# Four fused image layers on one core: new orders for copies, output products and the first loads

## The chip, the core and the metric

The kernel runs on one core of a Trainium2 chip. The metric is the device time of one execution in microseconds, the median of the runs. Everything is in 32-bit floats.

## What is computed

An input x of 4 batches, 512 channels and 64 x 64 places goes through four layers in turn. Cut to what matters:

```python
# layer 0: attention over the 4096 places, 64 channels of keys, queries and values
t = einsum('oc,bchw->bohw', w_qkv, x)
attn = softmax(einsum('bdk,bdq->bkq', key, query), axis=1)
x = scale * einsum('oc,bchw->bohw', w_out, einsum('bdk,bkq->bdq', value, attn)) + x
# layer 1: a router mixes 8 experts' weights for each batch; 1x1, 3x3 and 1x1 convolutions
rw = sigmoid(x.mean(axis=(2, 3)) @ router_w.T + router_b)
x = relu(bn(conv1(relu(bn(conv3(relu(bn(conv1(x)))))))) + x)
# layer 2: linear attention with softplus features
Q, K, V = softplus(Wq x + bq), softplus(Wk x + bk), Wv x + bv
x = x + gamma * (Q (K V)) / (Q . (sum K + 1e-6))
# layer 3: gate and scan; discounted running sums down the columns, then along the rows
gate, scan = split(w_proj x + b_proj)
x = x + gamma * gate * sigmoid(ds_cumsum(ds_cumsum(scan, d, 2), d, 3))
```

## The kernel before, in words

**Tiles.** A batch is held in SBUF as four *pairs*, tiles `x` of 128 partitions x 4 channel groups x 1024 places (2 MB each). The four batches run one after the other through `layer0` to `layer3` (loop at the end of `unshifted`). TensorE's order is the order of the program (`manual_schedule` for PE round that loop). In some scopes VectorE's or ScalarE's order is that of the program as well; elsewhere a scheduler orders their instructions by its own estimate of what is ready. In what follows "group" is a turn of the attention loop and "batch" one of the four images.

**Loads at the start.** `load_pair` (L86) loads a pair: for batch 0 the pairs 0 and 1 by channel group, four DMAs of 512 KB each (L91 to L93), the pairs 2 and 3 in one DMA of 2 MB (L95). Ahead of them SyncE issues the projection weights `wqkv_sb` (L100) and the parameters `prm_sb` (L102), behind them the other constants.

**Stage one of attention** (`Projections`, L213 to L338) makes keys, queries and values. For keys and queries it uses Strassen's seven products for two pairs at once; the lists in `steps` (L230) give the order, one list for the pairs (0, 1), one for (2, 3). The steps: a digit is one of the seven products on TensorE (eight matmul instructions, L305): 1, 6, 7 and 4 add up in the bank `y` (in the profile `kq`), 5 and 3 in the second half of `zy` (`kqz`), 2 in its first half. `seed` (L310) copies y into zy's first half, so that 2 adds to it; `e2` and `e3` (L313) copy y out in between. `c11` copies zy's first half into the key tile by four ScalarE copies (L291), `c22` (L327) and `c12` (L319) are VectorE's sums of zy's second half with e3 and e2, `c21` (L325) copies y to the queries. `t5` to `t4` and `n5` to `n4` are VectorE's differences of x that the products take (L253), t for this list, n for the next pairs. `v0` to `v3` are value products of a pair (16 instructions, L261); `v3a` and `v3b` are halves of one. `cp` copies values out (L267), `tr` transposes them (L274), `k` copies the second pair's keys to the other partitions. `zero` (L298) is a product of the identity whose result `seed` overwrites, put ahead of the first products while x is on its way.

**Attention** (L446 to L470): 16 groups, 0 to 15, four for each pair of queries. A group makes eight score tiles on TensorE (L367), each in one of three PSUM buffers (`pair_psum`, shared with all other two-bank tiles), ScalarE's exponentials into a ring of 12 tiles (L370), VectorE's running sum `acc` of them (L375, each waiting for the one before), and eight value products (`av`, L382), half a group behind. When a pair's last value product is done, its `sums` (`den` L398, reciprocal L401, `o` L410 or L412, range statistics L419 and L420) go into the list `late`, and for pairs 0 and 1 four output steps too (`y` L426, addition L431), each with the first group in which it may run. At the end of each group up to two of the list's items are taken (L468). Pair 3's own `den` is placed by hand, ahead of the value product with the index 121 of 128 (L456: `NPAIR * NT - 7`).

**Layer 2** leaves a rest in the list `left` (L830): the query features of the pairs 2 and 3, their `softplus` (L673: ScalarE's Abs, Relu, Exp, VectorE's +1, ScalarE's Ln, then `softplus_end`), and a division.

**Layer 3** works on eight tiles of two channel blocks by 1024 places. A tile has seven products for the scanned half (`s1` to `s7`) and, one turn later, seven for the gates (`g1` to `g7`), again in Strassen's way (L920), with ScalarE's copies in between (`seed` L925, `copy_out` L929, `first` L938, `third` L945). The scan of the tile before (`l`) runs beside: `rows` (VectorE, L953), `turn` (ScalarE, L959), `columns` (VectorE, L966 and L970), `sigmoid` (ScalarE, L975 and L976). The order is a list of rows: `first_steps` for the first tile, `steps` for the others, `last_steps`, and `end_steps` for the last batch's end. In a row `y` is the next output product of layer 2 (L838), `a` its addition to x (L843), `q` takes an item from `left`, `t` makes sums of x for the next pair or batch, `d` sets a scan constant.

**The range test** (L1114 to L1123) follows all batches: four small VectorE instructions on the statistics of all reciprocals, a product with ones (L1122), a conversion (L1123). Every engine then reads the result `fits` (L1514) and branches over the slower, general program (L1515).

The order of stage one, and the loop's end:

```python
first = "v1 cp01 5 1 seed v2 t6 t4 n5 6 n6 e2 2 7 e3 c22 c11 tr01 n7 4 c21 3 c12 n4"
if b == 0:
    first = "zero v0 1 seed t5 v1 cp01 t6 5 2 t7 t4 6 e2 v2 7 e3 n5 c22 c11 tr01 n6 n7 4 c21 3 c12 n4"
return first.split(), "5 1 seed k v3a 6 e2 2 v3b cp23 7 e3 c22 c11 tr23 4 c21 3 c12".split()
```

Of the kernel before, what the change touches and what calls it, by code (L numbers as in the profile page):

```python
# [15 lines left out]
P = 128  # L16
# [4 lines left out]
KC = C // P  # L21
# [25 lines left out]
def unshifted(ctx: ExitStack, tc: tile.TileContext, fits, x, wqkv_t, wout_t, router_t,  # L47
# [38 lines left out]
    def load_pair(b, pr):  # L86
        if b and pr == NPAIR - 1:
            places[NPAIR - 1:] = places[NPAIR], places[NPAIR - 1]
        t = places[pr]
        src = x[b, :, pr * 2 * NB:(pr + 1) * 2 * NB].rearrange("(kc p) n -> p kc n", p=P)  # L90
        if b == 0 and pr < 2:  # L91
            for kc in range(KC):
                nc.sync.dma_start(t[:, kc, :], src[:, kc, :])  # L93
        else:
            nc.sync.dma_start(t, src)  # L95
        return t
# [3 lines left out]
    nc.sync.dma_start(wqkv_sb, wqkv_t.rearrange("(kc p) o -> p kc o", p=P))  # L100
    prm_sb = const.tile([P, NPRM], F32, tag="prm", name="prm_sb")
    nc.sync.dma_start(prm_sb, prm)  # L102
# [110 lines left out]
    class Projections:  # L213
# [16 lines left out]
        def steps(self, b):  # L230
            first = "v1 cp01 5 1 seed v2 t6 t4 n5 6 n6 e2 2 7 e3 c22 c11 tr01 n7 4 c21 3 c12 n4"
            if b == 0:
                first = "zero v0 1 seed t5 v1 cp01 t6 5 2 t7 t4 6 e2 v2 7 e3 n5 c22 c11 tr01 n6 n7 4 c21 3 c12 n4"
            return first.split(), "5 1 seed k v3a 6 e2 2 v3b cp23 7 e3 c22 c11 tr23 4 c21 3 c12".split()
# [47 lines left out]
        def products(self, xs, pair, steps, key, qry, vt):  # L282
# [10 lines left out]
            for step in steps:  # L293
                if y is None and (step.isdigit() or step == "zero"):
                    y, zy = bank(f"kq_{self.b}_{pair[0]}"), pair_psum(f"kqz_{self.b}_{pair[0]}")
                if step == "zero":

                    nc.tensor.matmul(zy[:, 0, :].rearrange("p (j c) -> p j c", c=P), ident,  # L298
                                     ident[:, None, :].to_broadcast([P, TPB, P]), start=True, stop=True)
                elif step.isdigit():  # L300
                    k = int(step)
                    to = y if k in (1, 6, 7, 4) else zy[:, 0 if k == 2 else 1, :]
                    for c in range(2):
                        for h in range(2):
                            nc.tensor.matmul(to[h * D:(h + 1) * D, :], self.w[k][:, c, :],  # L305
                                             self.term(xs, pair, k, c)[:, h * NB:(h + 1) * NB],
                                             start=c == 0 and k in (1, 5), stop=c == 1,
                                             skip_group_check=k not in (1, 5))
                elif step == "seed":
                    nc.scalar.copy(zy[:, 0, :], y)  # L310
                elif step in ("e2", "e3"):
                    e[step] = block(f"{step}_{self.b}_{pair[0]}")
                    nc.scalar.copy(e[step], y)  # L313
                elif step == "c11":
                    to_key(lambda h, n0: zy[h * D:(h + 1) * D, 0, :], pair[0])
                elif step == "c12":
                    for h in range(2):
                        r, n0 = slice(h * D, (h + 1) * D), (2 * pair[1] + h) * NB
                        nc.vector.tensor_tensor(key[r, n0:n0 + NB], zy[r, 1, :], e["e2"][r, :], ALU.add)  # L319
                    self.left.append(lambda: to_key(lambda h, n0: key[h * D:(h + 1) * D, n0:n0 + NB], pair[1],  # L320
                                                    own=False))
                elif step == "k":
                    self.key_copies()
                elif step == "c21":
                    nc.vector.tensor_copy(qry[:, pair[0] * NB:(pair[0] + 1) * NB], y)  # L325
                elif step == "c22":
                    nc.vector.tensor_tensor(qry[:, pair[1] * NB:(pair[1] + 1) * NB], zy[:, 1, :], e["e3"], ALU.add)  # L327
                elif step[0] in "tn" and step[1].isdigit():
                    for c in range(2):
                        self.sum(xs, pair if step[0] == "t" else (2, 3), int(step[1]), c)  # L330
                elif step[:2] == "cp":
                    self.value_copy(int(step[2]) // 2)
                elif step[:2] == "tr":
                    self.value_turn(int(step[2]) // 2, vt)
                elif step[2:] == "a" or step[2:] == "b":
                    self.value(xs, int(step[1]), 0 if step[2] == "a" else 2, 2)
                else:
                    self.value(xs, int(step[1]))  # L338

    def layer0(b, xs, pro):  # L340
# [106 lines left out]
        with tc.manual_schedule(engines={mybir.EngineType.Activation}):  # L447
            for g in range(NPAIR * NT // ROUND):
# [6 lines left out]
                while done < (g + 1) * ROUND - (RING - ROUND):  # L455
                    if done == NPAIR * NT - 7:  # L456
                        inverse_sums(NPAIR - 1)
# [10 lines left out]
                for _ in range(2):  # L468
                    if late and late[0][0] <= g:
                        late.pop(0)[1]()  # L470
# [181 lines left out]
    def layer2(b, xs, sums_of_six, mix_last, conv2, conv3, wcq, qs):  # L652
# [20 lines left out]
        def softplus(w, pair, z):  # L673
# [7 lines left out]
            nc.scalar.activation(ln, u, AF.Ln)  # L681
            return lambda: softplus_end(w, pair, e, u, pos, ln)
# [99 lines left out]
        with tc.manual_schedule(engines={mybir.EngineType.DVE}):  # L782
# [39 lines left out]
            for i in range(2):  # L822
# [8 lines left out]
                lambda: left.append(softplus(*late)), lambda: left.pop()(),  # L831
# [36 lines left out]
    def layer3(b, xs, value_product, value_add, left, weights, wcq):  # L868
# [109 lines left out]
        class Gates(Block):  # L978
# [32 lines left out]
            def add_x(self, i, h=None):  # L1011
# [18 lines left out]
        first_steps = (("s1", "s seed", "q"), ("s5", "q"), ("s6", "s copy_out 2"), ("s2", "s first", "q"),  # L1030
                       ("s7", "s copy_out 3", "s fourth", "y"), ("s4", "s third", "a", "d"), ("y", "a", "q"),
                       ("s3", "s second"))
# [4 lines left out]
        end_steps = (("s1", "s seed", "l rows 1", "l rows 0"), ("g1", "l turn 1", "g seed"),  # L1037
# [11 lines left out]
        with tc.manual_schedule(engines={mybir.EngineType.DVE, mybir.EngineType.Activation}):  # L1049
# [9 lines left out]
            for i in range(len(tiles) + 1):  # L1059
# [7 lines left out]
                for step in first_steps if i == 0 else end_steps if "h" in who else steps if who["s"] else last_steps:  # L1067
                    for what in step:
# [37 lines left out]

    with tc.manual_schedule(engines={mybir.EngineType.PE}):
# [6 lines left out]
    ends = small.tile([P, 2], F32, tag="ends", name="ends", bufs=1)  # L1114
    nc.vector.tensor_reduce(ends[:, 0:1], stat[:, 0, :], AX.X, ALU.add)
    nc.vector.tensor_reduce(ends[:, 1:2], stat[:, 1, :], AX.X, ALU.min)
    fit = small.tile([P, 2], F32, tag="fit", name="fit", bufs=1)
    nc.vector.tensor_scalar(fit[:, 0:1], ends[:, 0:1], 1.0 / SUM_LO, None, ALU.is_le)
    nc.vector.tensor_scalar(fit[:, 1:2], ends[:, 1:2], 1.0 / SUM_HI, None, ALU.is_ge)
    nc.vector.tensor_tensor(fit[:, 0:1], fit[:, 0:1], fit[:, 1:2], ALU.mult)  # L1120
    cnt = bank("cnt", (1, 2))
    nc.tensor.matmul(cnt, fit[:, 0:1], ones[:, 0:2], start=True, stop=True)  # L1122
    nc.vector.tensor_copy(fits, cnt)  # L1123


@with_exitstack
def general(ctx: ExitStack, tc: tile.TileContext, x, wqkv_t, wout_t, router_t,
# [27 lines left out]
    nc.scalar.dma_start(wqkv_sb, wqkv_t.rearrange("(kc p) o -> p kc o", p=P))  # L1155
# [411 lines left out]
```

## Time and profile before

| | us |
|---|---|
| median of 3 runs (lowest, highest) | 2680.13 (2679.41, 2680.30) |
| the profiled execution | 2678.12 |
| its span, first to last instruction | 2676.2 |
| TensorE busy | 2643.2 |
| VectorE busy | 2016.3 |
| ScalarE busy | 1314.3 |
| DMA, mean rate over the span | 42 GB/s |
| last matmul starts | 2667.48 |
| last VectorE instruction ends | 2670.59 |

All times in the profile are counted from the span's first instruction. A line of the timeline has the start and the time taken in us, the engine, the kernel's line, the operation, what it writes and reads, its shapes and how many instructions were merged; in brackets stands how long the engine sat idle before it and what released it. A line of the waits names who waited for whom, the sum in us, how often, and the longest. PE is TensorE's products, PEld its weight loads, ACT ScalarE, DVE VectorE, POOL GpSimd, SP SyncE. The clock that TensorE was granted was full from 13.30 us on.

### The profile page before, as it was taken

Reading aid. Unit: us, or ns where it says so; the run is one execution under the profiler, and the core shown is the slowest. Engines: PE = TensorE matmul, PEld = TensorE weight load, DVE = VectorE, ACT = ScalarE, POOL = GpSimd, SP = SyncE. Lnnn points to the kernel's source line nnn. Section 1 sums busy time; section 2 is a strip of 40 time slices with the busy share of each in tenths; the row PEclk is TensorE's granted clock in tenths of the full one; section 3 lists DMA queues with packets and bytes.
Section 4 is the critical chain, followed back from the end, with each engine's and each line's share of the span. In section 5 each row is a group of like instructions: output and inputs, shape, how many; then the busy total and the mean of one; then the engine's idle time right before and its main releaser. Section 6 shows DMA issues by size and latency. Waiting matters only on the chain.

```text
span 2676.2 us, 25813 instructions
## 1 busy us (share of the span) xinstructions
PE 2643.2 (99%) x10048; PEld 1114.9 (42%) x10048; DVE 2016.3 (75%) x2272; ACT 1314.3 (49%) x1510; POOL 12.9 (0%) x26
## 2 busy tenths in 40 slices
PE   8999999999999999999999999999999999999998
PEld 2333364344333345434433334543443333554443
DVE  6777766788777776688877778668886777856787
ACT  3655353455555435345455553535555555263545
POOL 1000000000000000000000000000000000000000
PEclk9999999999999999999999999999999999999999
DMA  5000210022200021002220002101121000210001
GB/s 191 1 1 1 102 32 1 16 110 79 79 1 1 1 102 32 1 33 93 79 79 1 1 1 102 32 1 63 63 87 71 0 1 15 88 32 1 32 40 57
DMA packets 34883, 115.17 MB, mean 43 GB/s; under 512 B 3008, under 2 KB 12224, under 8 KB 33216
## 3 DMA queue, kind: packets, MB, share of 16 engines
q1 hardware_dynamic: 34752, 113.43, 11.4%
q8 instruction: 81, 1.33, 0.2%
q14 instruction: 50, 0.41, 0.1%
HBM read 79.86 MB, written 33.55 MB: 42 GB/s over the span
## 4 chain that ended last, share of the span: by engine, by line
PE 81%; DVE 11%; ACT 3%; issue 2%; DMA 1%; DVEq 0%; SPq 0%; ACTq 0%
PE av L382 14%; PE sx L920 14%; PE s L367 13%; PE zy L920 10%; DVE acc L375 4%; PE z L664 4%; PE c L639 4%; PE c L567 4%; PE c L616 3%; PE wv L838 2%; PE g L740 2%; PE xtr L725 2%; PE y L426 2%; PE c2e L616 2%; PE kqz L305 1%
## 5 line engine op out<-in xcount | busy, mean ns | idle before, releaser
L367 PE MATMUL s<-qv,key 64*128 64x512 f32 x2048 | 460.1, 596 | 0.9
L370 ACT ACTIVATE ring<-s 128x1024 f32<-128x1024 f32 x336 | 316.7, 1048 | 252.9 <-PE s L367 252.5
L375 DVE TENSOR_TENSOR acc<-acc,ring 128x1024 f32<-128x1024 f32 x312 | 381.7, 1223 | 59.2 <-ACT ring L370 31.3
L382 PE MATMUL av<-ring,qv 128*64 128x512 f32 x1344 | 302.2, 595 | 0.0
L367 PEld LDWEIGHTS s<-qv,key 64*128 64x128 f32 x2048 | 190.7, 186 | 265.3 <-issue 128.6
L920 PE MATMUL sx<-t,x 128*128 128x512 f32 x512 | 238.2, 599 | 2.2 <-ACT e L929 2.2
L375 DVE TENSOR_TENSOR acc<-acc,x 128x1024 f32<-128x1024 f32 x168 | 205.5, 1223 | 31.6 <-ACT x L370 15.5
L370 ACT ACTIVATE x<-s 128x1024 f32<-128x1024 f32 x176 | 167.1, 1053 | 124.9 <-PE s L367 124.6
L382 PEld LDWEIGHTS av<-ring,qv 128*64 128x64 f32 x1344 | 92.6, 137 | 200.1 <-issue 200.1
L925 ACT COPY zy<-sx 128x512 f32<-128x512 f32 x64 | 36.5, 570 | 258.0 <-PE sx L920 248.4
L382 PE MATMUL av<-x,qv 128*64 128x512 f32 x704 | 159.6, 595 | 0.0
L920 PEld LDWEIGHTS sx<-t,x 128*128 128x128 f32 x512 | 94.7, 190 | 134.1 <-issue 121.5
L970 DVE TENSOR_TENSOR_SCAN t<-x,t 128x512 f32<-128x512 f32 x128 | 149.2, 1209 | 1.6
L959 ACT COPY t<-s 128x1024 f32<-128x1024 f32 x64 | 127.6, 1993 | 43.9 <-DVE s L953 43.4
L953 DVE TENSOR_TENSOR_SCAN s<-wc,s 128x512 f32<-128x512 f32 x128 | 146.1, 1203 | 1.7 <-ACT s L945 1.7
L929 ACT ACTIVATE e<-sx,prm_sb 128x512 f32<-128x512 f32 x128 | 86.9, 686 | 107.0 <-PE sx L920 106.9
L976 ACT ACTIVATE s<-t 128x1024 f32<-128x1024 f32 x64 | 125.8, 1988 | 11.1 <-DVE t L970 11.1
L920 PE MATMUL zy<-t,wq 128*128 128x512 f32 x256 | 118.5, 602 | 0.5 <-ACT s L938 0.5
L920 PE MATMUL sx<-t,wq 128*128 128x512 f32 x256 | 117.0, 597 | 1.3 <-ACT e L929 1.3
L920 PE MATMUL sx<-x,wq 128*128 128x512 f32 x256 | 117.1, 595 | 0.0
L920 PE MATMUL zy<-x,x 128*128 128x512 f32 x256 | 116.3, 594 | 0.0
L920 PE MATMUL zy<-x,wq 128*128 128x512 f32 x256 | 115.9, 592 | 0.0
(227 smaller groups left out, 3451.1 us busy)
## 6 DMA issues: line engine op xcount, KB each, us to landing
out_dram<-s SPq DMA_DIRECT2D x62, 512.0 KB, 2.6
x<-in_x_dram SPq DMA_DIRECT2D x14, 2048.0 KB, 8.6
ex<-in_packed_dram SPq DMA_DIRECT2D x4, 2048.0 KB, 7.3
ex<-in_experts_dram SPq DMA_DIRECT2D x4, 2048.0 KB, 7.8
wq<-in_wproj_t_dram SPq DMA_DIRECT2D x32, 256.0 KB, 4.8
ex<-in_packed_dram SPq DMA_DIRECT2D x4, 1536.0 KB, 6.0
ex<-in_experts_dram SPq DMA_DIRECT2D x4, 1536.0 KB, 6.5
x<-in_packed_dram SPq DMA_DIRECT2D x4, 1536.0 KB, 7.6
```

Of the source, the lines that this page charges most:

```text
L367: nc.tensor.matmul(s[:, h, :], key[r, kt * P:(kt + 1) * P], qry[r, pr * NB:(pr + 1) * NB], start=True, stop=True)
L370: nc.scalar.activation(p, s, AF.Exp)
L375: nc.vector.tensor_tensor(accs[pr], accs[pr], p, ALU.add)
L382: nc.tensor.matmul(avs[pr][h * D:(h + 1) * D, :], vt[:, kt, :], ring[i % RING][:, h, :], start=kt == 0, stop=kt == NT - 1)
L567: nc.tensor.matmul(y[:, h, :], wc[:, kc, :], xs[pr][:, kc, h * NB:(h + 1) * NB], start=kc == 0, stop=kc == KC - 1)
L616: nc.tensor.matmul(y[:, lo - a:hi - a], u, v[:, lo:hi], start=dy == 1, stop=dy == 2)
L639: nc.tensor.matmul(y[:, h, :], wc[:, KC + 9 + m, :], h2[:, h, :], start=True, stop=True)
L920: nc.tensor.matmul(y, w[:, c, self.kind, self.j * P:(self.j + 1) * P], v[:, c, :], start=c == 0 and k in (1, 5), stop=c == 1, skip_group_c ...
L953: nc.vector.tensor_tensor_scan(self.half(i, h), along[:, self.j + 2 * i, :], self.half(i, h), 0.0, ALU.mult, ALU.add)
L959: nc.scalar.copy(self.t[i].rearrange("p (w r) -> p w r", w=W), self.s[i].rearrange("p (r w) -> p w r", w=W))
L970: nc.vector.tensor_tensor_scan(th, down[:, i, :], th, 0.0, ALU.mult, ALU.add)
L976: nc.scalar.activation(self.s[i].rearrange("p (r w) -> p w r", w=W), tw, AF.Sigmoid)
```

## The change

1. *Start.* `wqkv_sb` and `prm_sb` are issued by ScalarE, and the weights lie in DRAM in the order in which SBUF holds them (3 KB in a row for a partition, not 768 bytes). All four pairs of batch 0 are loaded by channel group. The first batch's list takes values and products 1 and 2 channel by channel (`v0:0` is one channel group of the value product, `1:0` one half of product 1); `zero` is done twice.
2. *Stage one.* Product 2 and `c11` come ahead of 6 and `e2`; value products are split in halves; `k` comes behind `tr23`.
3. *Attention.* One item of `late` a group, not up to two; pair 3's `den` two value products later.
4. *Layer 3.* The logarithm of `softplus` is an item of its own, taken behind the first tile's `copy_out 2`; the sigmoids' table is loaded by hand at the end of the first tile; in `steps` the second output product and its addition each come one product later; in `end_steps` the turns of the tile before come later.
5. *Range test.* It is done in the last batch, between `layer1` and `layer2`.

The diff, cut to its core:

```diff
-        if b == 0 and pr < 2:
+        if b == 0:
...
-    nc.sync.dma_start(wqkv_sb, wqkv_t.rearrange("(kc p) o -> p kc o", p=P))
+    nc.scalar.dma_start(wqkv_sb, wqkv_t)
...
-    nc.sync.dma_start(prm_sb, prm)
+    nc.scalar.dma_start(prm_sb, prm)
...
-            first = "v1 cp01 5 1 seed v2 t6 t4 n5 6 n6 e2 2 7 e3 c22 c11 tr01 n7 4 c21 3 c12 n4"
+            first = "v1 cp01 5 1 seed v2a t6 2 c11 t4 n5 6 v2b e2 n6 7 e3 c22 tr01 n7 4 c21 3 c12 n4"
             if b == 0:
-                first = "zero v0 1 seed t5 v1 cp01 t6 5 2 t7 t4 6 e2 v2 7 e3 n5 c22 c11 tr01 n6 n7 4 c21 3 c12 n4"
-            return first.split(), "5 1 seed k v3a 6 e2 2 v3b cp23 7 e3 c22 c11 tr23 4 c21 3 c12".split()
+                first = ("zero v0:0 1:0 v0:1 1:1 seed v0:2 2:0 v0:3 2:1 c11 t5 v1:0 v1:1 5 t6 v1:2 v1:3 cp01 t7 6 e2 "
+                         "v2:0 v2:1 t4 7 e3 c22 tr01 n5 4 c21 n6 3 c12 n7 v2:2 v2:3 n4")
+            return first.split(), "5 1 seed v3a 2 c11 6 v3b e2 cp23 7 e3 c22 tr23 k 4 c21 3 c12".split()
...
-                    if done == NPAIR * NT - 7:
+                    if done == NPAIR * NT - 5:
...
-                for _ in range(2):
-                    if late and late[0][0] <= g:
-                        late.pop(0)[1]()
+                if late and late[0][0] <= g:
+                    late.pop(0)[1]()
...
-            nc.scalar.activation(ln, u, AF.Ln)
-            return lambda: softplus_end(w, pair, e, u, pos, ln)
+            def logarithm():
+                nc.scalar.activation(ln, u, AF.Ln)
+                return lambda: softplus_end(w, pair, e, u, pos, ln)
+            return logarithm if in_parts else logarithm()
...
-                lambda: left.append(softplus(*late)), lambda: left.pop()(),
+                lambda: left.append(softplus(*late, in_parts=True)), lambda: left.append(left.pop()()),
+                lambda: left.pop()(),
...
-                 ("s6", "s copy_out 2", "l columns 0", "y"), ("g6", "g copy_out 2", "l sigmoid 1", "a"),
-                 ("s2", "l sigmoid 0", "s first"), ("g2", "g first", "t 0 1"),
+                 ("s6", "s copy_out 2", "l columns 0"), ("g6", "g copy_out 2", "l sigmoid 1", "y"),
+                 ("s2", "l sigmoid 0", "s first", "a"), ("g2", "g first", "t 0 1"),
...
-        first_steps = (("s1", "s seed", "q"), ("s5", "q"), ("s6", "s copy_out 2"), ("s2", "s first", "q"),
+        first_steps = (("s1", "s seed", "q"), ("s5", "q"), ("s6", "s copy_out 2", "q"), ("s2", "s first", "q"),
...
-                       ("s3", "s second"))
+                       ("s3", "s second", "sigmoids"))
...
-        end_steps = (("s1", "s seed", "l rows 1", "l rows 0"), ("g1", "l turn 1", "g seed"),
-                     ("s6", "s copy_out 2", "l columns 1"), ("s2", "l turn 0", "s first"),
-                     ("s7", "s copy_out 3", "l columns 0", "l sigmoid 1"), ("s5", "s fourth"),
+        end_steps = (("s1", "s seed", "l rows 1", "l rows 0"), ("g1", "g seed"),
+                     ("s6", "s copy_out 2", "l turn 1", "l columns 1"), ("s2", "s first"),
+                     ("s7", "s copy_out 3", "l turn 0", "l columns 0", "l sigmoid 1"), ("s5", "s fourth"),
...
+                        elif name == "sigmoids":
+                            tc.keep_in_program_order(nc.scalar.preload_act_table_set("sigmoid_and_others"))
...
             convs = layer1(b, xs, *layer0(b, xs, pro))
+            if b == B - 1:
+                all_in_range()
             xs, pro = layer3(b, xs, *layer2(b, xs, *convs))
```

`all_in_range` holds the lines of the range test, unchanged.

More of the change, by code (lines that the diff above doesn't have):

```diff
@@ L293, in products @@
             for step in steps:
+                step, _, channels = step.partition(":")
                 if y is None and (step.isdigit() or step == "zero"):
@@ L296, in products @@
                 if step == "zero":
-                    nc.tensor.matmul(zy[:, 0, :].rearrange("p (j c) -> p j c", c=P), ident,
-                                     ident[:, None, :].to_broadcast([P, TPB, P]), start=True, stop=True)
+                    for _ in range(2):
+                        nc.tensor.matmul(zy[:, 0, :].rearrange("p (j c) -> p j c", c=P), ident,
+                                         ident[:, None, :].to_broadcast([P, TPB, P]), start=True, stop=True)
                 elif step.isdigit():
@@ L302, in products @@
                     to = y if k in (1, 6, 7, 4) else zy[:, 0 if k == 2 else 1, :]
-                    for c in range(2):
+                    for c in (int(channels),) if channels else range(2):
                         for h in range(2):
@@ L334, in products @@
                     self.value_turn(int(step[2]) // 2, vt)
+                elif channels:
+                    self.value(xs, int(step[1]), int(channels), 1)
                 elif step[2:] == "a" or step[2:] == "b":
@@ L671, in features, with softplus @@
             return lambda: softplus(w, pair, z)
-        def softplus(w, pair, z):
+        def softplus(w, pair, z, in_parts=False):
             i = 2 * (len(kts) // 2 % 2)
@@ L1105, in layer3, with all_in_range @@
         return nxt, pro
+    def all_in_range():
+        ends = small.tile([P, 2], F32, tag="ends", name="ends", bufs=1)
+        nc.vector.tensor_reduce(ends[:, 0:1], stat[:, 0, :], AX.X, ALU.add)
+        nc.vector.tensor_reduce(ends[:, 1:2], stat[:, 1, :], AX.X, ALU.min)
+        fit = small.tile([P, 2], F32, tag="fit", name="fit", bufs=1)
+        nc.vector.tensor_scalar(fit[:, 0:1], ends[:, 0:1], 1.0 / SUM_LO, None, ALU.is_le)
+        nc.vector.tensor_scalar(fit[:, 1:2], ends[:, 1:2], 1.0 / SUM_HI, None, ALU.is_ge)
+        nc.vector.tensor_tensor(fit[:, 0:1], fit[:, 0:1], fit[:, 1:2], ALU.mult)
+        cnt = bank("cnt", (1, 2))
+        nc.tensor.matmul(cnt, fit[:, 0:1], ones[:, 0:2], start=True, stop=True)
+        nc.vector.tensor_copy(fits, cnt)
     with tc.manual_schedule(engines={mybir.EngineType.PE}):
@@ L1110, in unshifted @@
             convs = layer1(b, xs, *layer0(b, xs, pro))
+            if b == B - 1:
+                all_in_range()
             xs, pro = layer3(b, xs, *layer2(b, xs, *convs))
[L1114 to L1123, printed above, removed]
 @with_exitstack
@@ L1154, in general @@
     wqkv_sb = const.tile([P, KC, 3 * D], F32, tag="wqkv", name="wqkv_sb")
-    nc.scalar.dma_start(wqkv_sb, wqkv_t.rearrange("(kc p) o -> p kc o", p=P))
+    nc.scalar.dma_start(wqkv_sb, wqkv_t)
     xs = load_x(0)
@@ L1544 @@
         "x": a["x"].reshape(B, C, HW),
-        "wqkv_t": a["L0_conv_w_qkv"].T,
+        "wqkv_t": a["L0_conv_w_qkv"].T.reshape(KC, P, 3 * D).transpose(1, 0, 2),
         "wout_t": a["L0_conv_w_out"].T,
```

## The prediction

> **What bounds the kernel now.** I read the page's busy times first, then the waits of TensorE, then the stretches of the timeline round each wait.
>
> ```profile
> PE 2643.2 (99%) x10048; PEld 1114.9 (42%) x10048; DVE 2016.3 (75%) x2272; ACT 1314.3 (49%) x1510; POOL 12.9 (0%) x26
> ```
>
> TensorE is the bound: 33 us of the span are free. No product is removed, so the change can win only what TensorE waits. All its waits:
>
> ```profile
> PE kqz L305 <- ACT key L291: 8.4, 8, 1.6
> PE den L398 <- DVE acc L375: 5.0, 4, 1.2
> PE vv L261 <- DMA x<-in_x_dram: 3.6, 2, 2.9
> PE sx L920 <- ACT e L929: 3.6, 9, 1.4
> PE kqz L298 <- POOL ident masks.py:199: 1.5, 1, 1.5
> PE xtr L725 <- DVE xt L727: 0.9, 4, 0.2
> PE zy L920 <- ACT s L938: 0.5, 1, 0.5
> ```
>
> Each line gives microseconds, times, longest. A stall costs more than its gap: pairs of matmuls start 0.43 us apart (eight starts, one Strassen product, take 1.72)[...]. By spacing of starts, the eight kqz stalls cost 10.1 us, the four den stalls 1.39 each. About 9 us lie behind the last matmul, and the start is slow:
>
> ```profile
> 0.75 0.45 SPq L100 DMA_DIRECT2D wqkv_sb<-in_wqkv_t_dram  x1
> 6.41 1.97 PE L261 MATMUL vv<-x,wqkv_sb 128*64 128x512 f32 x4 [2.87 <-DMA x<-in_x_dram]
> 9.10 4.87 PE L261 MATMUL vv<-x,wqkv_sb 128*64 128x512 f32 x12 [0.71 <-DMA x<-in_x_dram]
> 13.79 1.88 PE L305 MATMUL kq<-x,wqkv_sb 128*64 128x512 f32 x8
> ```
>
> Four matmuls take as long before 13.3 us as eight do after it.
>
> [...] full clock is granted at 13.30, 4.2 us after TensorE last had to wait. [...]
>
> **Part 1, the start and the first batch: -5.4 us.** wqkv, 384 KB in 768-byte runs, lands at 3.97; the chunks of x of the first pair land behind it at 6.27, 9.05, 10.31, 11.60. In 3 KB runs on ACT's queue, beside x, I estimate 0.8 us less for it, so the fourth chunk lands at 10.8. TensorE takes per chunk two half products (0.86 each at full clock, 1.72 at half); from about 5.2, with the clock released at 9 to 10, all of v0, 1 and 2 are done at about 13.7. Before, at 13.36 only v0 was. From there the work left is 39.7 (all of stage one) - 6.9 = 32.8, switches 0.6, and 0.9 for step 5, which writes zy and so waits for c11's four copies (2.35 us, behind two half products of 1.72): stage one ends at 48.0; it ended at 53.4. Ends: clock only at 13.3, -3.0; clock at 8.6 and no wait at 5, -7.5. SP issues six DMAs more (16 for x, not 10); that delays the constants, first read at 78 us, and the experts, read at 300. ACT's two issues (0.5 each) lie before its first activation, which idled 3.0. The second zero matmul lies in the wait for x.
>
> **Part 2, c11 right behind product 2, batches 2 to 4: -6.7.**
>
> ```profile
> 695.20 0.59 ACT L313 COPY e<-kq 128x512 f32<-128x512 f32 x1 [2.85 <-PE kq L305]
> 696.54 2.35 ACT L291 COPY key<-kqz 64x512 f32<-64x512 f32 x4 [0.76 <-DVE qv L327]
> ```
> ```profile
> 698.95 1.51 PE L305 MATMUL kqz<-x,kqw 128*64 128x512 f32 x6 [0.91 <-ACT key L291]
> ```
>
> Product 3 waits for copies that start only after e3 and c22. Moved up they end 7 us before product 3. Six stalls: 8.15 by spacing, less what a normal start takes, -7.2. Late next is e2, now behind the copies on ACT: after product 2 the copies need 2.55, e2 0.58, together 3.13, while TensorE has product 6 and half a value product, 3.43; margin 0.3. I give 0.5 back. The key copies of step k move behind tr23, still before the scores. Ends: -7.2, and -3.6 if e2 is late each time.
>
> **Part 3, one output step a group: -3.9.** A group is 8 scores and 8 value products, 14.1 us. Two output products in a row hold two of the three score buffers until VectorE's 1.28 us additions have read them; the third score after them starts late at 141.2, 157.3, 202.5 and 218.6. By spacing this costs 1.36 a batch, 5.4 in all. With one product a group the third score needs its buffer 1.7 us after that product, enough unless VectorE is behind. It is behind after the group that follows a `sums`: there I leave 0.2 a time (8 times). Ends: -5.4, and +5.8 if all eight groups stall 0.35.
>
> **Part 4, the last group of attention: +3.9.** The four steps of pairs 0 and 1 now take groups 5 to 8 and 10 to 13, so `sums(2)` slips from the end of group 12 to that of 14, and its VectorE work falls into group 15. What it did to group 13:
>
> ```profile
> 246.06 3.36 DVE L401 RECIPROCAL rec<-den 128x512 f32<-128x512 f32 x1 [2.71 <-PE den L398]
> 250.42 0.68 DVE L410 SCALAR_TENSOR_TENSOR o<-avsb,rec 128x512 f32<-128x512 f32 x1
> 251.02 0.68 DVE L419 TENSOR_REDUCE stat<-rec 128x1 f32<-128x512 f32 x1
> 251.62 0.68 DVE L420 TENSOR_REDUCE stat<-rec 128x1 f32<-128x512 f32 x1
> 253.53 7.87 DVE L375 TENSOR_TENSOR acc<-acc,ring 128x1024 f32<-128x1024 f32 x6
> ```
>
> Group 13 began at 245.95, its last acc ended at 261.40, +15.45. Group 15, undisturbed, began at 274.12:
>
> ```profile
> 286.93 1.08 PE L398 MATMUL den<-acc,ones 128*64 128x512 f32 x4 [1.24 <-DVE acc L375]
> ```
>
> den starts at +12.81 where TensorE was free at +11.42. With -5 for -7 two value products more (1.71) go first: free at +13.14. Undisturbed, the wait (1.39) is gone; with `sums(2)` in the way den starts at +15.5 and waits 2.36: +0.97 a batch. The reciprocal behind it (3.36) is covered by the five value products left (4.3). Ends: -5.6 (no disturbance) and +4.5. I take the disturbance, because group 13 shows it.
>
> **Part 5, layer 3: -4.9.** [...] In the first tile copy_out 2 (L929) stands behind the logarithm (1.06 us); put ahead of it, TensorE's start at 471.46 is 0.48 earlier. In the second tile stands:
>
> ```profile
> 495.60 1.28 ACT L976 ACT_TABLE_LOAD   x1
> 501.14 1.26 ACT L929 ACTIVATE e<-sx,prm_sb 128x512 f32<-128x512 f32 x2
> ```
>
> and TensorE waits for these copies at 501.88, 0.6 by spacing. Loaded at the end of the first tile, the table falls into the 5 us that ACT idles before 482.13. The second output product at 518.92 waits for the addition of the first (0.14); one product (1.72) later it doesn't. 1.22 x 4. The additions keep their place behind the columns' scans on VectorE. Ends: -2.5 and -5.8.
>
> **Part 6, the end: -1.5.** Turns behind the copies save TensorE 2.2 (stalls at 2637.36 and 2639.82), but the last 12.4 us are VectorE's, from 2658.15, which waits for ACT's sigmoid: followed through ACT and VectorE that chain gains 0.8. The range test moved into batch 4: VectorE had its operands ready at 2311.8, 12 us before TensorE comes to it, so it costs 0.3 there. At the end, TensorE's branch (4.0 us) and the engines' reads of `fits` no longer wait for the test; the last store, 3.6 us where the one before took 2.0, may land earlier: 0.7 net. Ends: -0.1 and -3.5.
>
> **Sum.** -5.4 - 6.7 - 3.9 + 3.9 - 4.9 - 1.5 = -18.5 against the profiled execution, 2678.1 (span 2676.2 and 1.9 round it): 2659.6. The median of the runs lies 2.0 above that execution: **2661.6**.
>
> **Rivals.**
> - *den is covered*: VectorE's sums of group 15 go ahead of the rest of `sums(2)`. Part 4 gives -5.6: 2652.1. For: the order there is the scheduler's, not written out. Against: in group 13 the rest went first. 0.22.
> - *The waits only move*: all low ends with part 4 as taken, -3.0 - 3.6 + 0 + 3.9 - 2.5 - 0.1 = -5.3: 2674.8. For: margins of 0.3 at e2 and 0.1 at the scores. 0.14.
> - *Slower*: c11, always released by VectorE before (0.76 above), goes on waiting for it, now for the sum n6 that ends at 695.89. Then the copies, e2 behind them and product 7 come 5.6 late (698.9, not 693.3): 3 x 5.6 + 3.8 of part 2 + 5.4 of part 1 lost, +26.0 - 18.5 = +7.5: 2687.6. It turns the sign from 4 us a batch. Against: what released it is c22, which the new lists put behind it. 0.04.
> - *Nothing is won*, about 2680: 0.05.
>
> **Chances.** Forecast 0.55, the rest as given. 0.2% (5.4 us) is about what a measurement tells from none. Faster 0.90, same 0.06, slower 0.04. The range 2651 to 2671 holds the forecast, nearly all of the first rival and a part of the second.
>
> **What would show it.** First real matmul near 5.2, scores near 48. No wait of kqz for key; if kqz or kq waits for e, part 2's margin was too small. den waits for acc about 2.4 (part 4), or not at all. No table load within the second tile, no wait of sx for e but in the end. The forecast fails upward if new waits of TensorE name ACT in stage one, downward if den does not wait.

## The result and the profile after

| | before | after |
|---|---|---|
| median of the runs, us (lowest, highest) | 2679.89 (2678.67, 2680.30) | 2661.66 (2660.56, 2661.85) |
| the profiled execution | 2678.12 | 2661.49 |
| its span | 2676.2 | 2659.6 |

The ratio is 0.9932, with a 95% interval of 0.9919 to 0.9945: by the medians 18.2 us less, where 18.5 were forecast. The busy times on the page of the changed kernel:

```profile
PE 2637.0 (99%) x10050; PEld 1117.6 (42%) x10050; DVE 2019.8 (76%) x2272; ACT 1315.4 (49%) x1510; POOL 11.0 (0%) x26
```

The two instructions more are the second `zero`. What changed is what TensorE waits for. All its waits after:

```profile
PE den L405 <- DVE acc L382: 8.9, 4, 2.2
PE kqz L303 <- POOL ident masks.py:199: 1.5, 1, 1.5
PE vv L263 <- DMA wqkv_sb<-in_wqkv_t_dram: 1.0, 1, 1.0
PE xtr L733 <- DVE xt L735: 0.9, 4, 0.2
PE kqz L310 <- ACT key L293: 0.8, 1, 0.8
PE zy L929 <- DVE s L951: 0.8, 1, 0.8
```

Held against the list of before: seven of the eight waits of `kqz` for the keys are gone, all waits of `sx` for `e` too, and the wait of `den`, 5.0 us in four times before, has grown to 8.9.

A wait in such a list is shorter than what it costs (the 2.21 us of `den` in batch 1 cost 2.37 by the spacing of starts), so I cut the span at TensorE's own marks instead: the first products of keys, of scores, of the router's logits, and so on, in each batch. A stage has the same products before and after, so the difference of two intervals is what the change won or lost there. With the prediction's parts beside it:

| part | predicted | measured | where |
|---|---|---|---|
| 1, start and first batch | -5.4 | -3.8 | first scores at 49.76, not 53.53 |
| 2, c11 behind product 2 | -6.7 | -7.2 | first keys to first scores, batches 2 to 4: 31.63 each, not 33.88, 34.09, 34.12 |
| 3, one output step a group | -3.9 | -5.5 | first scores to logits 240.1, not 240.4 (batch 1: 241.67, not 242.33), -1.6 in all, and part 4 taken out; 0.35 of it is a score at 55.60 in batch 1 before, ahead of all output steps |
| 4, the last group | +3.9 | +3.9 | `den` starts 0.98 later behind the product before it, four times |
| 5, layer 3 | -4.9 | -4.9 | first output product to last product 221.39, not 222.61, a batch |
| 6, the end | -1.5 | -0.95 | last batch -1.30 more, range test +0.31 in batch 4, behind the last product +0.04 |
| half clock behind the last `den` | none | +1.7 | batch 4, scores to logits 241.80, not 240.10 |
| sum | -18.5 | -16.6 | span 2659.6, not 2676.2 |

The start in the timeline of TensorE, after (start, time taken, what; in brackets the idle time and its releaser):

```profile
1.46 3.78 PE L303 MATMUL kqz<-ident 128*128 128x512 f32 x4 [1.46 <-POOL ident masks.py:199]
6.27 1.98 PE L263 MATMUL vv<-x,wqkv_sb 128*64 128x512 f32 x4 [1.03 <-DMA wqkv_sb<-in_wqkv_t_dram]
8.03 1.92 PE L310 MATMUL kq<-x,wqkv_sb 128*64 128x512 f32 x4
```

The first real product waited for the weights until 6.27, not 5.2, and four matmuls still take 1.92 there, where four take 1.02 from 11.06 on: half clock. Full clock came at 10.66. The fourth chunk of x landed at 10.16 (10.8 forecast, 11.60 before), so the later chunks were not late.

Stage one of batch 2 on ScalarE, and on TensorE:

```profile
684.48 2.36 ACT L293 COPY key<-kqz 64x512 f32<-64x512 f32 x4 [2.94 <-PE kqz L310]
686.86 0.59 ACT L318 COPY e<-kq 128x512 f32<-128x512 f32 x1
```
```profile
685.90 1.89 PE L263 MATMUL vv<-x,wqkv_sb 128*64 128x512 f32 x8
687.62 1.89 PE L310 MATMUL kq<-ring,kqw 128*64 128x512 f32 x8
```

The copies are now released by TensorE's product 2 and by nothing else. `e2` ends at 687.45, and product 7 starts at 687.62 without idle time in front: the margin that the prediction put at 0.3 is 0.17, and holds.

The end of attention on VectorE, and `den` on TensorE:

```profile
272.09 1.16 DVE L382 TENSOR_TENSOR acc<-acc,ring 128x1024 f32<-128x1024 f32 x1
273.17 0.68 DVE L417 SCALAR_TENSOR_TENSOR o<-avsb,rec 128x512 f32<-128x512 f32 x1
273.78 0.68 DVE L426 TENSOR_REDUCE stat<-rec 128x1 f32<-128x512 f32 x1
274.37 0.68 DVE L427 TENSOR_REDUCE stat<-rec 128x1 f32<-128x512 f32 x1
...
278.94 5.21 DVE L382 TENSOR_TENSOR acc<-acc,x 128x1024 f32<-128x1024 f32 x4
```
```profile
284.21 1.08 PE L405 MATMUL den<-acc,ones 128*64 128x512 f32 x4 [2.21 <-DVE acc L382]
```

`o` and the two statistics of pair 2 stand in the middle of pair 3's running sum, as in group 13 before. The last `acc` ends at 284.15, and `den` had been free to start 2.21 us earlier.

### The profile page after: what moved, and what is told of

Read it like the earlier page. It is cut to its first block, busy times and chain, and to the rows that moved or that the text cites. A ratio compares the mean times of both kernels' runs of the same rounds, so it can differ in the third digit from the quotient of the medians.

```text
span 2659.6 us, 25807 instructions
## 1 busy us (share of the span) xinstructions
PE 2637.0 (99%) x10050; PEld 1117.6 (42%) x10050; DVE 2019.8 (76%) x2272; ACT 1315.4 (49%) x1510; POOL 11.0 (0%) x26
## 4 chain that ended last, share of the span: by engine, by line
PE 96%; DVE 2%; issue 1%; ACT 1%; DMA 0%; DVEq 0%; ACTq 0%
PE sx L929 16%; PE av L389 16%; PE s L374 16%; PE zy L929 12%; PE z L670 4%; PE c L645 4%; PE c L573 4%; PE c L622 3%; PE wv L847 2%; PE y L433 2%; PE kq L310 2%; PE vv L263 2%; PE g L748 2%; PE xtr L733 2%; PE kqz L310 2%; PE c2e L622 2%
## 5 line engine op out<-in xcount | busy, mean ns | idle before, releaser
L374 PE MATMUL s<-qv,key 64*128 64x512 f32 x2048 | 453.8, 593 | 0.0
L929 PE MATMUL sx<-t,x 128*128 128x512 f32 x512 | 232.4, 593 | 0.0
```

The source lines that it names most:

```text
L374: nc.tensor.matmul(s[:, h, :], key[r, kt * P:(kt + 1) * P], qry[r, pr * NB:(pr + 1) * NB], start=True, stop=True)
L929: nc.tensor.matmul(y, w[:, c, self.kind, self.j * P:(self.j + 1) * P], v[:, c, :], start=c == 0 and k in (1, 5), stop=c == 1, skip_group_c ...
```

## Experiments

All are edits of the changed kernel; times and ratios are against the kernel before, run on the same chip.

| run | median us (lowest, highest) | before, same chip | ratio, 95% interval |
|---|---|---|---|
| two_items | 2653.92 (2653.61, 2654.45) | 2678.66 | 0.9910 (0.9895 to 0.9925) |
| sums_first | 2653.29 (2651.97, 2654.37) | 2678.66 | 0.9908 (0.9893 to 0.9924) |
| old_lists | 2668.53 (2665.74, 2672.44) | 2678.66 | 0.9960 (0.9946 to 0.9974) |
| weights_first | 2660.71 (2657.63, 2661.84) | 2678.66 | 0.9933 (0.9920 to 0.9947) |
| one_zero | 2661.34 (2659.63, 2663.50) | 2677.96 | 0.9941 (0.9925 to 0.9958) |
| table_late | 2659.57 (2658.36, 2660.93) | 2677.96 | 0.9934 (0.9917 to 0.9950) |
| log_ahead | 2663.57 (2662.67, 2664.58) | 2677.96 | 0.9948 (0.9932 to 0.9965) |
| old_end | 2661.87 (2661.16, 2662.50) | 2677.96 | 0.9941 (0.9925 to 0.9958) |
| den_after | 2654.30 (2653.48, 2656.29) | 2678.60 | 0.9912 (0.9898 to 0.9925) |
| best | 2648.99 (2648.20, 2650.38) | 2678.60 | 0.9891 (0.9876 to 0.9906) |
| y_back | 2660.60 (2656.89, 2662.08) | 2678.60 | 0.9936 (0.9921 to 0.9951) |
| test_last | 2660.81 (2660.59, 2660.88) | 2678.60 | 0.9935 (0.9920 to 0.9951) |

Runs of one kernel spread by up to 7 us, more than several of these edits are worth. For those the verdict is the interval between marks in the trace. Where no stretch at half clock falls in it or just ahead of it, and nothing in it was edited, it repeats to 0.02 us in batches 2 to 4.

### Parts 3 and 4: is it sums(2) that makes den wait?

**two_items** gives the list two items a group again.

```diff
-                if late and late[0][0] <= g:
-                    late.pop(0)[1]()
+                for _ in range(2):
+                    if late and late[0][0] <= g:
+                        late.pop(0)[1]()
```

> The changed kernel, but with up to two items of the list a group again (pair 3's den stays two value products later). Theory (VectorE's work of sums(2) in group 15 makes den wait): sums(2) falls back to the end of group 12, den no longer waits, 2.4 us by spacing less in each batch (-9.5 in all), and the half-clock stretch behind the last batch's den goes too (-1.7); in return the third score after each couple of output products stalls again (1.3 a batch, +5.2). Together -6.0: about 2655.7. Rival (den waits for another reason, for instance because it stands too early still): den still waits about 2.2, only the stalls come back, 2666 to 2667.

Measured: 2653.92. `den` does not wait at all, and single scores start late again: four in batch 1 (at 134.90, 151.00, 196.22 and 212.32) come 0.61 to 0.66 behind the one before, where 0.43 is usual. The interval from scores to logits falls to 239.3, 238.9 and 239.0 in batches 2 to 4; over the four batches that is 4.2 us, where 9.5 - 5.2 = 4.3 were expected. The rest by which this profile is shorter is the half clock behind `den`, 1.7, and an earlier full clock (6.71, first scores at 47.57). More is won at `den` than is lost at the scores, so part 3 as made costs more, through part 4, than it brings.

**sums_first** keeps one item a group and puts `sums` at the head of the list.

```diff
-                        late.append((g, lambda pr=pr: sums(pr)))
+                        late.insert(0, (g, lambda pr=pr: sums(pr)))
```

> The changed kernel, but a pair's sums go to the head of the list, ahead of output products still in it: sums(2) runs at the end of group 12, the last output product at the end of group 14. Theory: the 5.5 us of sums(2) are caught up by group 15; only that output product's addition (1.28) is in the way, den waits about 0.8 instead of 2.2 and no score stalls: -1.5 a batch, and no half-clock stretch, -1.7: about 2654. Rival (one output product a group keeps VectorE behind anyway): den waits about 2 as before, 2661 to 2662.

Measured: 2653.29. Its waits have, and its VectorE has in the last group:

```profile
PE den L405 <- DVE acc L382: 2.2, 4, 0.5
```
```profile
269.75 5.21 DVE L382 TENSOR_TENSOR acc<-acc,ring 128x1024 f32<-128x1024 f32 x4
275.06 5.21 DVE L382 TENSOR_TENSOR acc<-acc,x 128x1024 f32<-128x1024 f32 x4
```

No reciprocal and no statistics stand before these eight additions: `sums(2)` was done two groups earlier. 240.1 becomes 238.85, 238.48 and 238.49 (the first holds one late score, at 851.52). That comes near what the prediction's first rival describes ("den is covered", 9.5 us better than the forecast), though by moving `sums(2)` and not by the scheduler's order within group 15; the four intervals give 6.1 of it, since `den` still waits 0.54. What delays `den` is shown: the place of `sums(2)`.

**den_after** leaves the list and puts `den` behind the loop, one value product later.

```diff
-                    if done == NPAIR * NT - 5:
-                        inverse_sums(NPAIR - 1)
...
+        inverse_sums(pr)
         for i in range(done, NPAIR * NT):
```

> The changed kernel with pair 3's den moved one value product further, to behind the loop of the groups. Theory (den waits for VectorE's running sum, which does not care where den stands): the wait of den falls from 2.21 to 1.35 us, first scores to the router's logits takes 239.2 us a batch instead of 240.1, 3.4 us in all. A wait of 1.35 us is also too short for the second theory's price, that a wait of more than about 2.0 us inside one clock window (3.41 us, whose grid all the traces fit) halves the clock for the next window and costs 1.7 us: no stretch at half clock behind den. Ratio to before about 0.992 or a little under. Rival (the reciprocal behind den is then no longer covered by four value products): the logits wait for it, the interval stays at 240.1, nothing is won.

Measured: 2654.30, interval 239.25 in batches 2 to 4, that is -0.85.

```profile
PE den L405 <- DVE acc L382: 5.4, 4, 1.4
```

The reciprocal stays covered. Of the 6.8 by which this profile's span is shorter than that of the changed kernel, 3.4 are this; 1.9 came from an earlier full clock (7.42, first scores at 47.90), and 1.7 from the absence of half clock behind `den`. Why both vary comes below.

**best** does both.

> The sums first in the list, and den one value product later. Theory: with the sums first den waited 0.54 us, which cost 0.92 by spacing; one value product (0.86) later it does not wait, the interval from the first scores to the logits goes from 238.5 to about 237.6, 3.6 us in all against the kernel with the sums first alone: ratio to before about 0.9895. Rival (reciprocal uncovered, or the product left behind waits for ScalarE's ring): a new wait of the logits or of av takes the place, ratio 0.991 as with the sums first alone.

Measured: 2648.99, the fastest of all; the intervals 237.72 in batches 3 and 4 (expected 237.6) and 238.08 in batch 2, where one score comes late, at 852.58.

```profile
276.73 5.75 PE L389 MATMUL av<-ring,qv 128*64 128x512 f32 x26
282.31 1.03 PE L405 MATMUL den<-acc,ones 128*64 128x512 f32 x4
283.17 3.60 PE L389 MATMUL av<-x,qv 128*64 128x512 f32 x16
```

TensorE goes through `den` without idle time on either side. Against sums_first that is 0.77 a batch; against the changed kernel without its half clock the four intervals are 9.2 shorter, nearly the 9.5 of the rival.

### Part 2: the order of stage one

**old_lists** gives batches 2 to 4 their lists of before.

```diff
-            first = "v1 cp01 5 1 seed v2a t6 2 c11 t4 n5 6 v2b e2 n6 7 e3 c22 tr01 n7 4 c21 3 c12 n4"
+            first = "v1 cp01 5 1 seed v2 t6 t4 n5 6 n6 e2 2 7 e3 c22 c11 tr01 n7 4 c21 3 c12 n4"
...
+            second = "5 1 seed k v3a 6 e2 2 v3b cp23 7 e3 c22 c11 tr23 4 c21 3 c12"
```

> The changed kernel, but batches 2 to 4 have the old lists of stage one (product 2 behind e2, c11 behind c22). Theory: the six stalls of kqz for key come back, 2.25 + 2.46 + 2.49 us as the two traces stand apart from a stage's first product to its first score: +7.2, about 2668.9. Rival (the gain came from splitting the value products or from the place of k, and the stalls only moved): less than half of that, below 2665.5.

Measured: 2668.53. The waits of before are back, in the list and in the timeline of TensorE:

```profile
PE kqz L313 <- ACT key L296: 8.7, 7, 2.2
```
```profile
693.89 2.56 PE L313 MATMUL kqz<-x,kqw 128*64 128x512 f32 x8 [2.21 <-ACT key L296]
696.23 3.01 PE L313 MATMUL kqz<-ring,wqkv_sb 128*64 128x512 f32 x8
```

Keys to scores takes 36.89, 34.23 and 34.70 instead of 31.63. Of the 36.89, about 1.7 are half clock again: the second line's eight matmuls take 3.01, not 1.89. Without it 9.2 us come back, 2.0 more than the 7.2. These 2.0 are another wait: the copies follow a sum of VectorE (`c22`), and ahead of it VectorE now waits 1.24, 0.27 and 0.75 us for a load of x, where the kernel before shows such a wait in batch 4 alone (0.15). Part 2 is shown: the stalls come back with the old lists. Which of their differences does it (product 2 and `c11` moved, values split, `k` moved) was not taken apart; that the copies are now released by product 2 and not by `c22` speaks for the first.

### Part 1: loads and clock

**weights_first** issues the weights on SyncE's queue, ahead of x.

```diff
-    nc.scalar.dma_start(wqkv_sb, wqkv_t)
+    nc.sync.dma_start(wqkv_sb, wqkv_t)
```

> The changed kernel, but SyncE issues the projection weights, in their new layout, ahead of x; ScalarE issues the parameters only. Theory ([...] the weights land only when as much of x has landed, at 6.23 in the changed kernel, and they are what the first product waits for): weights at about 3.5, first chunk of x at 5.3 to 5.6, first value product near 5.5 and not 6.27, later chunks as before; stage one about 0.4 to 0.9 shorter, 2660.8 to 2661.3. Rival (the amount of bytes is what counts, the order is not): first chunk at 6.2 or later, the time the same or up to 0.5 longer.

**one_zero** takes the second product of the identity away.

```diff
-                    for _ in range(2):
+                    for _ in range(1):
```

> The changed kernel, but with one zero product at the start, as before. Theory [...]: TensorE idles from 3.5 to 6.3, the clock is granted one window later, at about 14 and not 10.66; up to 3.4 us at half clock more, +1.7 us on stage one: about 2663.4. Rival (the clock comes with the work behind 6.27 alone): full clock at 10.7 again, no difference.

Measured: 2660.71 and 2661.34; neither differs from the changed kernel (2661.66) by more than runs spread. In weights_first the weights land at 4.08, the first chunk of x at 5.53, the first product starts at 5.67. With both queues the weights land at 5.57 to 6.48 and the chunk 0.17 to 0.23 before them, in every profile of that start. In the changed kernel the two queues move packets side by side: between 2 and 5 us 126 on SyncE's (0.49 MB) and 115 on ScalarE's (0.34 MB). My 0.8 us for the landing was an estimate with no measured number under it, since in the kernel before SyncE's queue alone carried both. Nor did the rows of 3 KB bring the weights sooner: issued first on SyncE's queue they land at 4.08 here, with the parameters on the other queue beside them, and at 3.97 before. The other edits of the start (loads by channel group, products by channel) were not taken apart.

Full clock came at 4.38 in weights_first and at 10.80 in one_zero, and I first took that for the edits' doing. It is not: table_late, whose start is the changed kernel's, had it at 4.45 and the first scores at 47.22 (weights_first 47.25), while the changed kernel itself had 10.66 and 49.76 (one_zero 49.65). The last section shows what decides this. The 1.7 us expected of one_zero was an estimate, and whether the second product of the identity helps no run shows. In one_zero two would not have helped, by my estimate: the two windows that did not release the clock had 2.07 and 1.45 us of busy time, with a second product about 2.5 and 2.7, and one of 2.75 did not release it either (last section). Elsewhere it does, I estimate from the same windows: one such product keeps TensorE busy for 2.07 us, two for 3.78 (the changed kernel), and the least busy window that released the clock had 2.79. Of the twelve profiles with two, six had full clock by 5.87, and the four matmuls of these products are all that the windows before it held.

### Part 5: layer 3

**log_ahead** puts the logarithm ahead of `copy_out 2` again.

```diff
-                lambda: left.append(softplus(*late, in_parts=True)), lambda: left.append(left.pop()()),
-                lambda: left.pop()(),
+                lambda: left.append(softplus(*late)), lambda: left.pop()(),
```

> The changed kernel with the logarithm of the rest of layer 2 ahead of the first tile's copy_out 2 again. Theory: product 7 of the first tile waits 0.2 for that copy, 0.48 by spacing, four times: +1.9, about 2663.6. Rival (something else released it): 2661.7.

Measured: 2663.57, and 0.48 more in layer 3 in each of the four batches (221.87, not 221.39), the prediction's number.

```profile
PE sx L928 <- ACT e L937: 0.8, 4, 0.2
```
```profile
465.06 1.06 ACT L688 ACTIVATE ln<-sp 128x1024 f32<-128x1024 f32 x1 [0.76 <-DVE sp L686]
466.03 0.67 ACT L937 ACTIVATE e<-sx,prm_sb 128x512 f32<-128x512 f32 x1
```

**table_late** drops the table load at the end of the first tile.

```diff
-                       ("s3", "s second", "sigmoids"))
+                       ("s3", "s second"))
```

> The changed kernel without the early load of the sigmoids' table, which falls back ahead of the second tile's sigmoid. Theory: the copies behind it come 1.28 us later and the second tile's product 4 waits for them, 0.6 by spacing, four times: +2.4, about 2664.1. Rival (moving the second output product had already taken the wait away, so the table is covered): no wait of sx for e, 2661.7.

Measured: 2659.57, and exactly 221.39 in layer 3: nothing lost. My theory had put 0.6 a batch on the table, and it fell here. The table is back among the sigmoids, yet the copy behind them is in time:

```profile
486.91 1.28 ACT L985 ACT_TABLE_LOAD   x1
488.20 1.97 ACT L985 ACTIVATE s<-t 128x1024 f32<-128x1024 f32 x1
489.98 0.26 ACT L984 COPY wc<-t 128x64 f32<-128x64 f32 x1
490.13 1.98 ACT L985 ACTIVATE s<-t 128x1024 f32<-128x1024 f32 x1
491.91 0.65 ACT L947 ACTIVATE s<-zy,prm_sb 128x512 f32<-128x512 f32 x1
492.45 0.68 ACT L938 ACTIVATE e<-sx,prm_sb 128x512 f32<-128x512 f32 x1
```

The product that needs `e` starts at 493.95 and does not wait. **y_back** is the other half: table early, output product back in its old row.

```diff
-                 ("s6", "s copy_out 2", "l columns 0"), ("g6", "g copy_out 2", "l sigmoid 1", "y"),
-                 ("s2", "l sigmoid 0", "s first", "a"), ("g2", "g first", "t 0 1"),
+                 ("s6", "s copy_out 2", "l columns 0", "y"), ("g6", "g copy_out 2", "l sigmoid 1", "a"),
+                 ("s2", "l sigmoid 0", "s first"), ("g2", "g first", "t 0 1"),
```

> The changed kernel with the second output product of layer 2 and its addition back in their old rows; the sigmoids' table still early. Without the early table, with the product moved, nothing was lost (221.39 us from the first output product to the last product of layer 3 in both). Theory A (either of the two alone ends the wait of the first tile's second half): only the 0.14 of the product that waits for the addition comes back, 221.5 us. Theory B (the move of the product did it, the table is worth nothing): the wait of sx for e comes back as before, 221.39 + 0.74 = 222.1 us.

Measured: 221.39 again. Theory A holds, and goes further than I had it: not even the 0.14 comes back.

```profile
487.45 0.69 ACT L938 ACTIVATE e<-sx,prm_sb 128x512 f32<-128x512 f32 x1 [2.29 <-PE sx L929]
...
492.60 0.69 ACT L938 ACTIVATE e<-sx,prm_sb 128x512 f32<-128x512 f32 x1
494.31 0.69 ACT L938 ACTIVATE e<-sx,prm_sb 128x512 f32<-128x512 f32 x1 [1.03 <-PE sx L929]
```

In ScalarE's order the sigmoids stand behind one copy `e` of the second tile and ahead of the next. From the start of the first of these copies to that of the next, ScalarE needs 6.42 us with the table (486.03 to 492.45 in table_late; 494.72 to 501.14 before) and 5.15 without (487.45 to 492.60). The output product, when it stands ahead of the products that the first copy waits for, holds that copy back by its own 1.05; behind them, it gives ScalarE that time. Either of the two edits is enough. Before, with neither, ScalarE's lateness also held VectorE (5.97 idle at 500.83), and with it the addition that the later output product waited for: the 0.6 and the 0.14 were one delay.

### Part 6: the end

**old_end** restores the last batch's rows, with the turns ahead of the copies.

```diff
-        end_steps = (("s1", "s seed", "l rows 1", "l rows 0"), ("g1", "g seed"),
-                     ("s6", "s copy_out 2", "l turn 1", "l columns 1"), ("s2", "s first"),
-                     ("s7", "s copy_out 3", "l turn 0", "l columns 0", "l sigmoid 1"), ("s5", "s fourth"),
+        end_steps = (("s1", "s seed", "l rows 1", "l rows 0"), ("g1", "l turn 1", "g seed"),
+                     ("s6", "s copy_out 2", "l columns 1"), ("s2", "l turn 0", "s first"),
+                     ("s7", "s copy_out 3", "l columns 0", "l sigmoid 1"), ("s5", "s fourth"),
```

> The changed kernel with the old end_steps. Theory: TensorE's two stalls come back (2.2 us by spacing), but the last tiles' scans on VectorE and ScalarE set the end, so the time is longer by only 0.8 to 1.3: about 2662.8. Rival (TensorE sets the end): +2.2, 2663.9. Second rival (the scans alone set the end): the same time.

Measured: 2661.87, and the last batch's layer 3 takes 1.30 more (219.65, not 218.35). TensorE in old_end, and in the changed kernel:

```profile
2620.16 1.98 PE L929 MATMUL sx<-t,x 128*128 128x512 f32 x4 [1.38 <-ACT e L938]
2622.62 1.98 PE L929 MATMUL zy<-t,wq 128*128 128x512 f32 x4 [0.47 <-ACT s L947]
```
```profile
2628.30 1.98 PE L929 MATMUL zy<-x,x 128*128 128x512 f32 x4 [0.75 <-DVE s L951]
```

By spacing the two old waits cost 2.2, the new one, for VectorE, 0.9: 1.3 are kept. From the last product to VectorE's last end it is 3.6 in both, so all of it reaches the end; I had let 0.8 of it through.

**test_last** puts the range test behind all batches.

```diff
-            if b == B - 1:
-                all_in_range()
             xs, pro = layer3(b, xs, *layer2(b, xs, *convs))
+    all_in_range()
```

> The changed kernel with the range test behind all batches again. Prediction: 0.3 is won in batch 4 (logits to the first convolution 43.1, not 43.4) and 0.7 to 1.0 is lost behind the last product, where the change left the time as it was (9.3 us): 10.0 us or more there. Rival (the last store is longer than the test, so the test lay beside it): 9.3 us there again, and the kernel is 0.3 us faster for it.

Measured: 2660.81; 0.31 is won in batch 4 (43.09 from the logits to a product of the 3x3 convolution, not 43.40), and from the last product of layer 3 to the end it is 9.48, where the changed kernel has 9.31 and the one before 9.27. The last store decides that stretch: it landed 3.63 us after its issue before, 3.51 after, 3.68 in test_last, and between 2.7 and 4.1 in the other profiles, and the span ends 2.0 to 2.2 us behind the landing in these three. No interval shows a cost of the test there: the rival holds, and the move cost 0.3 for nothing. One thing did move. The two stores ahead of the last land in 2.0 us each before and in test_last, in 2.4 to 3.9 in the twelve profiles with the test in batch 4; and the last packets on queue q8 (of the kind `instruction` on the page) begin 5.1 and 5.3 us before the end in those two, 8.5 in the changed kernel. Whether the one has to do with the other was not shown.

## Why the prediction came out right

The median was forecast to 0.1 us, and that is partly luck. The sum was made for the profiled execution, 2659.6; it measured 2661.5. Then 2.0 was added because the median before lay that far above its profile; after, it lies 0.2 above. Two errors of about 1.9 cancelled.

- **Part 1, right in kind, 1.6 too large** in this profile. The term that failed is the landing of the weights: by my estimate they were to come 0.8 sooner than before, and they came at 6.23 (3.97 before), so the first product started at 6.27 and not 5.2, and the clock came at 10.66, not 9 to 10. In the 13 profiles of the changed kernel and its edits, the first scores start between 47.22 and 49.76: 48.0 was a fair middle, and no number for one execution. The wait of step 5 was 0.80 (0.9 forecast).
- **Part 2, right; the term of 0.5 for `e2` was not needed**, with 0.17 of margin.
- **Part 3, the term for VectorE's lag was wrong.** 0.2 was left for each of eight groups behind a `sums` (and 5.44 - 1.6 is 3.8, not 3.9); no score starts late in any group. Without the 0.35 at 55.60 part 3 brought 5.1, near the low end of -5.4.
- **Part 4, right**: 2.36 forecast and 2.37 found, both by spacing (2.21 of it idle), +0.97 and +0.98 a batch. Reading the new last group off the old group 13 carried the forecast. What the step left out is the clock: behind one of the four waits, in batch 4, it was half for 3.41 us.
- **Part 5, right in sum, wrong in its split.** 0.48 for the logarithm is shown. The 0.74 of the second tile has one cause with two cures, either enough.
- **Part 6, 0.55 short**: the end chain kept 1.3 of the 2.2 (0.8 forecast), the test cost its 0.3, and the 1.0 that it was to save at the tail (0.7 net) did not come.
- Of the rivals, "den is covered" did not happen; the kernel best gets there by two other edits and finds 9.2 of its 9.5 us. "The waits only move" was right in part 4 and in the new wait of 0.75 at the end; the new 0.8 of step 5 was in the forecast. `c11` waits for VectorE nowhere, so nothing speaks for the rival on the slower side.

## What to carry to other kernels

When a queue of small jobs is thinned, follow each job to its new place: what is harmless in group 13 delays the end when it lands in group 15, and a job that others wait for belongs at the head of the list. Where two edits are made at one stall, undo them one at a time before saying what each is worth. Edits worth less than a few microseconds are read from intervals between fixed marks of the trace, since a run's time also holds its start: in the 13 profiles here full clock came between 4.38 and 10.80 us.

## What the hardware showed that was not expected

**A wait of 2.2 us, shorter than a clock window of 3.41, halved the clock.** The changed kernel in stretches of 3.41 us round the last `den` (length, then busy time and instructions of TensorE, its weight loads, VectorE, ScalarE and GpSimd, then TensorE's granted clock, DMA share and rate):

```profile
2260.05:2263.46 3.41, 1.23 (x6) 0.48 (x8) 2.12 (x3) 0.00 (x0) 0.00 (x0) 1.00 0.00 0
2263.46:2266.87 3.41, 3.41 (x10) 0.97 (x8) 3.25 (x1) 0.00 (x0) 0.00 (x0) 0.50 0.23 35
2266.87:2270.28 3.41, 3.41 (x18) 1.16 (x16) 0.90 (x3) 0.00 (x0) 0.00 (x0) 1.00 1.00 404
```

Ten starts in the second stretch, 18 in the third. From the first grant of full clock, 10.664, to this loss, 2263.461, it is 660.0 times 3.4133 us; from the end of the half clock, 2266.874, to the next loss, 2655.993, behind the last product, 114.0 times; in the kernel before, from 13.302 to 2672.284, 779.0 times. In both traces the clock changed on one grid of 3.4133 us, whose steps are the windows here. In the window ahead of the loss at 2655.993 TensorE was idle throughout; ahead of the one at 2263.461, 2.18 us of idle time were enough. Nine of the profiles have such waits of 2.2 us, 37 in all. Ten have 2.04 us or more of idle time inside one window, and all ten are followed by a window at half clock; the other 27 are split by a window's edge, with 2.01 or less in either, and none is. Two that lie close, in test_last and in y_back:

```profile
940.84:944.26 3.42, 1.36 (x8) 0.51 (x10) 2.13 (x3) 0.00 (x0) 0.00 (x0) 1.00 0.02 5
944.26:947.67 3.41, 3.41 (x12) 0.97 (x10) 3.12 (x1) 0.00 (x0) 0.00 (x0) 0.50 0.33 62
```
```profile
278.22:281.63 3.41, 1.41 (x8) 0.24 (x4) 3.20 (x3) 0.00 (x0) 0.00 (x0) 1.00 0.18 76
281.63:285.05 3.42, 3.20 (x16) 1.20 (x18) 2.24 (x2) 0.00 (x0) 0.00 (x0) 1.00 0.10 17
```

1.36 us busy of 3.41 lost the clock (1.38 in old_lists, before 1609.83, did too), 1.41 kept it: a bound between 1.38 and 1.41, for these kernels and with the profile's modelled ends of matmuls. It divides all windows at full clock in the 14 profiles, those at the kernels' ends included. Each loss costs 1.70. From ten in 37, an estimate: 0.5 us a wait on average, 1.8 in the changed kernel, on top of what the waits of `den` show. Before, at 1.24 a wait, none came.

**The start draws from the same grid.** At half clock, a window with 2.79 us of busy time or more (sums_first) released it, one with 2.75 or less (log_ahead, 3.63 to 7.05) did not. So full clock came anywhere from 4.45 (table_late) to 10.66 us (the changed kernel) with the same first products, depending on where the grid lay and on when the weights landed: in table_late the window from 1.04 to 4.45 had 2.99 us of busy time, in the changed kernel those from 0.42 to 3.84 and from 3.84 to 7.25 had 2.38 each, the second with the wait of 1.03 for the weights in it. By the first scores that is worth 2.5 us (47.22 and 49.76), more than several of the edits above, and it is the reason why a first-batch gain can't be read from one profile.
